# Layer 3: a row of key tiles in two steps of 512 query columns instead of three

## Chip, core and metric

The kernel runs on one core of a Trainium2 chip. The time is the device time of one launch in microseconds; below 3281 us is one run of the whole program. A core has a matrix engine (TensorE, PE in the profile; its weight loads are PEld), a vector engine (VectorE, DVE), a scalar engine (ScalarE, ACT), GpSimd (POOL), a sequencer that issues transfers (SyncE, SP), and DMA engines. Each engine runs its own instructions in order and waits for the others by semaphores. SBUF is the working memory, PSUM the small memory that TensorE writes to, in banks of 512 float32 columns.

## What is computed

Four images of 256 channels and 48 x 48 pixels go through four residual layers: x = x + layer(group_norm(x)). Layers 0 to 2 are convolutions and are not touched. Layer 3 is a linear attention over square windows:

```python
q = sigmoid(Wq x); k = sigmoid(Wk x)        # 8 heads of 32 channels
v = Wv x / |Wv x|                           # per head
for w in (1, 2, 4):                         # windows of 48, 24 and 12 pixels
    ws = Hh // w
    wk = _box(Ik, ws, Hh, Ww)               # sums of k over each query's window
    wkv = _box(Ikv, ws, Hh, Ww)             # sums of k v^T over the same window
    attn = einsum('bdhw,bdfhw->bfhw', q, wkv)
    norm = einsum('bdhw,bdhw->bhw', q, wk)
    outs.append(attn / (norm + 1e-6))
out = Wout concat(outs) + bout
```

## The kernel before

**Tiles.** The image is cut into row blocks of RB = 8 rows (NRB = 6, NB = 384 pixels). A query block is one row block of one image `b` and one half `ct` of the channels (four heads, HG = 4): 48 blocks, in the list `order`. A key tile is one row block `a` times 16 columns (KC), so 128 keys, and a row block has three of them, c = 0, 1, 2 (NKC). A query sees a key tile if the tile lies inside one of its windows, half widths HALVES = 24, 12, 6.

**A step.** `stream` lists every (block, a, c). For each one the kernel does this:

- `scores`: for each of four heads, TensorE multiplies the key tile (32 channels x 128 keys) by the queries that can see it, into a PSUM tile `s` of two banks for two heads; there are two such tiles, and both are used in each step. The queries lie by rows (`qs`, r then w), so the columns that see the tile (`cols_seen`: 40, 48 or 40 of the 48) are cut out of each row: 320 or 384 columns a head.
- `unseen`: a small bfloat16 product adds a large negative number where a query does not see a key of the widest window.
- `masked`: ScalarE applies a relu to the widest window's part, and VectorE multiplies the middle window's part by a 0/1 mask; GpSimd takes the narrowest window's part from the middle one's result. All go to an SBUF tile `sm` (six buffers). If the rows lie whole within the widest window (`rows_whole`), only the strips at its edge (`strips`) are taken here, because the inside comes from sums of k v^T (`state`, `window_state`, `whole`); a middle tile then has two strips of 8 columns on both sides. For the farthest row blocks (distance 3) the whole tile goes through ScalarE for one pair of heads and VectorE for the other.
- `sums`, LAG = 2 steps later: TensorE multiplies `sm` by the values (128 keys x 32 channels) and adds into three PSUM tiles `acc`, one per window, four heads in four groups of 32 columns.

Row blocks are visited nearest first, with near tiles (those that the narrowest window sees) and far ones in turn (`tiles_of`).

**What fills the gaps.** Projections of the next image (`Projection`), prefix sums of k (`k_sums`), the norms (`norms`, `inverse`), key states (`state`), and the output product (`prepare`, `finish`) are generators. After each step `advance(time, pool_time)` lets each of them go on by one piece if the step's spare TensorE time (`bank`, `turn`) or GpSimd time (`pool_turn`) allows it. All of these share one PSUM bank (`ps_m`), one piece at a time. `until` runs them without new steps until something is made: a block's sums may not begin before the block two before it is done. All engines keep program order, so this planner's order is the order on the chip.

**Names in the profile.** A helper records the operations, so nearly all have line 208; they are told apart by tiles: `s`, `sm`, `acc`, `nhi` (norm sums), `nq` (queries for the norms), `pt` (prefix sums), `o` and `stage` (sums of the two channel halves), `rc` (1/norm), `out_ps`, `proj_ps`, `keys_ps`, `kv_ps`, `norm_ps`.

Of the kernel before, what the change touches and what calls it, by code (L numbers as in the profile page):

```python
# [22 lines left out]
P = 128  # L23
# [60 lines left out]
LAG = 2  # L84
HOLD = 1000
# [4 lines left out]
MCOL0 = [max(h, KC) for h in HALVES]  # L90
# [13 lines left out]
def strips(c):  # L104

    (c0, c1), (f0, f1) = cols_seen(0, c), cols_whole(c)
    return [(p0, p1) for p0, p1 in ((c0, f0), (f1, c1)) if p0 < p1]
# [10 lines left out]
def penalties():  # L118

    got = []  # L120
    for c in range(NKC):
        xs = np.concatenate([np.arange(p0, p1) for p0, p1 in strips(c)])
        got.append(((0, c), RB, np.tile(xs[None, :], (RB, 1)), None))
    for da, (r0, r1) in FAR_ROWS.items():
        for c in range(NKC):
            c0, c1 = cols_seen(0, c)
            rs = np.arange(r0, r1)
            got.append(((da, c), r1 - r0, np.tile(np.arange(c0, c1)[None, :], (len(rs), 1)), rs))
    return got


PENALTY_AT, _at = {}, 0
for _key, _nr, _xs, _ in penalties():
    PENALTY_AT[_key] = _at, _xs.size
    _at += _xs.size
# [5 lines left out]
SM_ROOM = 2 * RB * sum(min(W, n) for n in (KC, KC + 2 * HALVES[1], KC + 2 * HALVES[2]))  # L141


def window_masks():
# [5 lines left out]
    for h, nr, m0, ncol in list(zip(HALVES, MROWS, MCOL0, MCOLS))[1:]:  # L150
        qi = np.arange(nr) - h + 1
        qj = np.arange(ncol) - m0
        rows = (qi[None] - h <= ki[:, None]) & (ki[:, None] < qi[None] + h)
        cols = (qj[None] - h <= kj[:, None]) & (kj[:, None] < qj[None] + h)
        ms.append((rows[:, :, None] & cols[:, None, :]).reshape(P, -1))
# [4 lines left out]
    for (da, c), _, xs, rs in penalties():  # L160
        at, n = PENALTY_AT[da, c]
        kx = c * KC + np.arange(KC)[:, None, None]
        costs[RB : RB + KC, at : at + n] = (
            UNSEEN * ~((xs - h <= kx) & (kx < xs + h))
        ).reshape(KC, n)
        if rs is not None:
            ky, ys = da * RB + np.arange(RB)[:, None, None], rs[:, None] + 0 * xs
            costs[0:RB, at : at + n] = (
                UNSEEN * ~((ys - h <= ky) & (ky < ys + h))
            ).reshape(RB, n)  # L170
# [41 lines left out]
def conv_preact_kernel(  # L212
# [104 lines left out]
    def start(job):  # L317
        active.append([step + 1, job])
# [47 lines left out]
    free = {"xr": 2, "xn": 2, "kt": 2, "sq": 2, "vt": 1, "cs": 1, "o": 2, "rc": 2, "res": 2}  # L366

    FETCH = 4
# [22 lines left out]
    class Projection:  # L391
# [14 lines left out]
        def load(self, g, a, n):  # L406
# [7 lines left out]
            xr = self.scr.tile([P, NCT, RB, W], F32, tag="xr", name="xr")  # L414
# [27 lines left out]
        def qk(self, g, a, name, mo):  # L442
# [18 lines left out]
            rows = t.rearrange("p (r c x) -> p c r x", c=NKC, x=KC)  # L461
# [14 lines left out]
        def v(self, g, a, c):  # L476
# [24 lines left out]
            sq = self.scr.tile([P, HEADS, D], F32, tag="sq", name="sq")  # L501
# [14 lines left out]
            for _ in range(4):  # L516
                yield from pool_turn(n, 4)
                pool.tensor_mul(u, t, r)
                pool.tensor_mul(u, u, r)
                pool.tensor_scalar(u, u, -0.5, 1.5, ALU.mult, ALU.add)  # L520
                pool.tensor_mul(r, r, u)
                yield 1
# [1061 lines left out]
    with (  # L1584
# [16 lines left out]
                "p (r c) -> p r c", c=MCOLS[i]  # L1601
# [32 lines left out]
        def k_sums(b, a, mo):  # L1634

            yield from wait_for(("k", b, mo, a))
            kp = kps[mo]
            chans = slice(mo * P, (mo + 1) * P)
            sync.dma_start(
                out=shifted(kp, 0),  # L1640
                in_=kf_d[b][chans, a * NB : (a + 1) * NB].rearrange("p (r x) -> p r x", x=W),
            )
            yield 2 * FETCH
            yield from take("cs")
            cs = scr.tile([P, (RB + 1) * ROW], F32, tag="cs", name="cs", bufs=1)
            n = GAP + RB * ROW
            for i, j in ((0, n // 2), (n // 2, n)):
                dve.tensor_tensor_scan(
                    cs[:, i:j],
                    kp[:, i:j],  # L1650
                    kp[:, 0:1].to_broadcast([P, j - i]),
                    cs[:, i - 1 : i] if i > 0 else 0.0,
                    ALU.add,
                    ALU.add,
                )
                yield 1
            pt = scr.tile([P, NW, RB, W], F32, tag="pt", name="pt")
            for wi, h in enumerate(HALVES):
                dve.tensor_sub(pt[:, wi], shifted(cs, h - 1), shifted(cs, -h - 1))
                yield 1  # L1660
            free["cs"] += 1
            for r in range(RB):
                if r % 2 == 0:
                    yield from pool_turn(NW * W, 2)
                if a > 0 or r > 0:
                    up = pt[:, :, r - 1, :] if r > 0 else carry[:, mo]
                    pool.tensor_add(pt[:, :, r, :], pt[:, :, r, :], up)
            pool.tensor_copy(carry[:, mo], pt[:, :, RB - 1, :])
            yield 1
            sync.dma_start(  # L1670
                out=kb_d[b][:, chans, a * RB : (a + 1) * RB, :].rearrange("w p r x -> p w (r x)"),
                in_=pt.rearrange("p w r x -> p w (r x)"),
            )
            made.add(("kb", b, mo, a))

        def norms(b, rb):
# [4 lines left out]
            def load(ct):  # L1681
# [3 lines left out]
                qf = scr.tile([P, RB, W], F32, tag="nq", name="nq")  # L1685
                sync.dma_start(
                    out=qf.rearrange("p r w -> p (r w)"),
# [30 lines left out]
            for hi, lo, qf in loaded:  # L1718
# [5 lines left out]
                for wi in range(NW):  # L1724
                    yield from pool_turn(NB)
                    pool.tensor_mul(hi[:, wi], hi[:, wi], qf)
# [23 lines left out]
            nr = scr.tile([P, nn], F32, tag="nr", name="nr")  # L1750
# [13 lines left out]
        def load_kv(b, ct, a):  # L1764
# [11 lines left out]
            start(state(b, ct, a))  # L1776
# [40 lines left out]
        def load_q(b, ct, rb):  # L1817
            qs = qp.tile([P, RB, W], F32, tag="qs", name="qs")
            sync.dma_start(
                out=qs.rearrange("p r w -> p (r w)"),  # L1820
# [16 lines left out]
        class Block:  # L1837


            def __init__(self, b, ct, rb, qs):  # L1840
# [3 lines left out]
                    [(a, c) for a, c in self.tiles if seen(wi, a, rb)] for wi in range(NW)  # L1844
# [3 lines left out]
            def scores(self, pr, a, c):  # L1848
                rb = self.rb
                r0, r1 = rows_seen(0, a, rb)  # L1850
                c0, c1 = cols_seen(0, c)
                s = ps_s.tile([P, 2, 512], F32, tag="s", name="s")
                for j in range(2):
                    head = slice((2 * pr + j) * D, (2 * pr + j + 1) * D)
                    pe.matmul(
                        s[:, j, 0 : (r1 - r0) * (c1 - c0)],
                        kvs[self.b, self.ct, a][0][head, c, :],
                        self.qs[head, r0:r1, c0:c1],
                        start=True,
                        stop=False,  # L1860
                    )
                return s[:, :, 0 : (r1 - r0) * (c1 - c0)].rearrange(
                    "p j (r w) -> p j r w", w=c1 - c0
                )

            def unseen(self, ss, a, c):

                whole = rows_whole(a, self.rb)
                at, n = PENALTY_AT[(0 if whole else a - self.rb), c]
                ps = strips(c) if whole else [cols_seen(0, c)]  # L1870
                w, x0 = ps[0][1] - ps[0][0], cols_seen(0, c)[0]
                for pr, s in enumerate(ss):
                    for j in range(2):
                        g = 2 * pr + j
                        rows = slice(g * D, g * D + RB + KC)
                        cost = masks[rows, PEN_AT + at : PEN_AT + at + n]
                        dst = s[:, j, :, ps[0][0] - x0 : ps[-1][1] - x0]
                        if len(ps) == 1:
                            cost = cost.rearrange("p (r w) -> p r w", w=w)
                        else:  # L1880
                            step = (ps[1][0] - ps[0][0]) // w
                            cost = cost.rearrange("p (r s w) -> p r s w", w=w, s=2)
                            dst = dst.rearrange("p r (s w) -> p r s w", w=w)[:, :, ::step]
                        pe.matmul(dst, picks[rows, :], cost, start=False, stop=True)

            def masked(self, a, c, ss):

                rb = self.rb
                all0 = rows_seen(0, a, rb), cols_seen(0, c)
                (r0, r1), (c0, c1) = all0  # L1890
                wis = [wi for wi in range(NW) if seen(wi, a, rb)]
                full = rows_whole(a, rb)
                pieces = {wi: [cols_seen(wi, c)] for wi in wis}
                if full:
                    pieces[0] = strips(c)

                def room():

                    t = smp.tile([P, SM_ROOM], F32, tag="sm", name="sm")
                    at, got = 0, {}  # L1900
                    for wi in wis:
                        nr = rows_seen(wi, a, rb)[1] - rows_seen(wi, a, rb)[0]
                        for p0, p1 in pieces[wi]:
                            n = 2 * nr * (p1 - p0)
                            got[wi, p0] = t[:, at : at + n].rearrange(
                                "p (j r w) -> p j r w", j=2, r=nr
# [3 lines left out]
                    return got  # L1910
# [389 lines left out]
```

## Time and profile before

| | |
|---|---|
| median of 3 runs | 3281.37 us (3277.27 to 3284.92) |
| the profiled execution's own time | 3280.77 us |
| its span in the trace | 3279.0 us, mean TensorE clock 0.968 |
| first and last product of tile `s` | 1380.4 and 3261.4 us |
| last copy of `acc` | begins at 3265.4 us |
| busy share of the span: PE, DVE, ACT, POOL | 89%, 61%, 31%, 45% |
| records of `s`, of its mask products, of `acc` | 5760, 2880, 14976 |
| GpSimd operations on `sm` | 768, 606.9 us |
| VectorE mask operations on `sm` | 1152, 633.1 us |
| ScalarE operations on `sm` | 1680, 559.9 us |

A float32 product leaves two records in the trace, a bfloat16 one leaves one. In a group's line the numbers behind the bar are busy us, mean ns of one, and the engine's idle time just before them with what ended it. Busy time of TensorE overlaps itself: four heads' products run at once in four parts of the array.

### The profile page before, as it was taken

What the parts mean: (1) busy time and instruction counts of PE and PEld (TensorE: products, weight loads), DVE (VectorE), ACT (ScalarE), POOL (GpSimd) and SP (SyncE); (2) the same over time, 40 slices, a digit from 0 to 9 for tenths busy, and PEclk for the clock granted to TensorE, in tenths of its full rate; (3) what the DMA queues carried; (4) which work ended last, traced back from release to release, by engine and by line L of the source; (5) the groups of instructions that cost most, each with busy time, mean ns of one, the idle gap of its engine ahead of it and who ended that gap; (6) DMA issues with size and microseconds to landing.
All of it is one profiled execution on the core that took longest, in us unless ns stands there. A gap on an engine that the chain in (4) does not pass through costs nothing.

```text
span 3279.0 us, 90374 instructions
## 1 busy us (share of the span) xinstructions
PE 2927.0 (89%) x37898; PEld 1845.0 (56%) x37898; DVE 1989.5 (61%) x3571; ACT 1028.7 (31%) x2710; POOL 1476.0 (45%) x2402
## 2 busy tenths in 40 slices
PE   3678999898899978899999999989999999989998
PEld 2456777678676755755544544544455544455444
DVE  7886568648856633666666746665556564444444
ACT  0002210111121053255433344433345433334332
POOL 0000021003002121366899978887546896543433
PEclk9889899999999989899999999999999999999999
DMA  8746513432341253233646645655424555311321
GB/s 268 220 152 189 164 47 119 120 122 78 107 155 55 91 165 120 92 102 125 186 145 177 186 134 172 176 157 167 117 75 125 157 162 152 99 46 36 93 67 53
DMA packets 373099, 424.13 MB, mean 129 GB/s; under 512 B 129075, under 2 KB 328531, under 8 KB 371539
## 3 DMA queue, kind: packets, MB, share of 16 engines
q1 hardware_dynamic: 371491, 416.32, 41.3%
q8 instruction: 298, 4.88, 0.6%
q0 software_dynamic: 144, 1.24, 0.2%
q14 instruction: 110, 0.90, 0.1%
q10 hardware_dynamic: 1056, 0.79, 0.1%
HBM read 288.24 MB, written 131.25 MB: 128 GB/s over the span
## 4 chain that ended last, share of the span: by engine, by line
PE 58%; DVE 12%; POOL 7%; ACT 5%; issue 3%; DMA 3%; SPq 0%; ACTq 0%; POOLq 0%; DVEq 0%
PE s L208 17%; PE cv L208 15%; PE acc L208 12%; PE out_ps L208 5%; PE proj_ps L208 5%; DVE sm L208 4%; ACT sm L208 4%; POOL sm L208 3%; PE ap L208 2%; POOL pt L208 2%; DVE l2v L208 2%; POOL nhi L208 1%; DVE v L208 1%; PE keys_ps L208 1%; DVE x L208 1%
## 5 line engine op out<-in xcount | busy, mean ns | idle before, releaser
L208 DVE TENSOR_TENSOR sm<-s,masks 128x432 f32<-128x432 f32 (+8 forms) x1152 | 633.1, 577 | 551.0 <-PE s L208 477.4
L208 ACT ACTIVATE sm<-s 128x128 f32<-128x128 f32 (+3 forms) x1680 | 559.9, 361 | 903.2 <-PE s L208 708.8
L208 POOL TENSOR_TENSOR sm<-sm,masks 128x336 f32<-128x336 f32 (+8 forms) x768 | 606.9, 811 | 524.2 <-DVE sm L208 520.6
L208 PE MATMUL s<-qs,ks 32*128 32x320 f32 (+3 forms) x5760 | 649.3, 496 | 98.5 <-DVE sm L208 49.4
L208 PE MATMUL acc<-sm,vs 128*32 128x64 f32 (+13 forms) x14976 | 661.6, 303 | 4.4 <-POOL sm L208 4.3
L208 PE MATMUL cv<-vx,wt 128*128 128x288 f32 x2080 | 562.2, 426 | 92.3 <-DVE vx L208 51.2
L208 PEld LDWEIGHTS acc<-sm,vs 128*32 128x32 f32 x14976 | 348.9, 110 | 315.7 <-issue 237.7
L208 PEld LDWEIGHTS cv<-vx,wt 128*128 128x128 f32 x2080 | 404.1, 199 | 214.7 <-issue 54.4
L208 PEld LDWEIGHTS s<-qs,ks 32*128 32x128 f32 x5760 | 260.0, 183 | 397.2 <-ACT sm L208 168.3
L208 POOL MEMSET v<- 128x16 f32 (+1 forms) x120 | 18.5, 215 | 717.8 <-DVE vx L208 631.4
L208 PE MATMUL cv<-v,wl 128*128 128x384 f32 x1152 | 223.9, 354 | 24.3 <-DVE x L208 9.2
L208 DVE TENSOR_SCALAR sm<-s 128x672 f32<-128x672 f32 (+1 forms) x144 | 118.6, 824 | 190.1 <-PE s L208 167.8
L208 PEld LDWEIGHTS cv<-v,wl 128*128 128x128 f32 x1152 | 214.5, 195 | 34.1 <-issue 16.1
L208 PE MATMUL s<-masks 24*128 24x128 bf16 (+4 forms) x2880 | 215.2, 233 | 0.0
L208 POOL TENSOR_TENSOR pt<-pt 128x144 f32<-128x144 f32 x336 | 178.9, 532 | 21.8
L208 POOL TENSOR_TENSOR v<-l2v,v 128x384 fp32r<-128x384 f32 x96 | 109.0, 1166 | 125.3 <-ACT v L208 116.6
L208 POOL TENSOR_TENSOR nhi<-nhi,nq 128x384 f32<-128x384 f32 x144 | 152.6, 1078 | 0.0
L208 PE MATMUL cv<-pad,wl 128*128 128x384 bf16 x864 | 143.6, 328 | 0.0
L208 PEld LDWEIGHTS <-masks 24*128 24x128 bf16 x2880 | 100.8, 93 | 50.9 <-issue 1.0
L208 PE MATMUL out_ps<-o,wout_sb 128*32 128x384 f32 x1152 | 122.2, 492 | 2.3 <-DVE res L208 1.5
L208 PE MATMUL out_ps<-stage,wout_sb 128*32 128x384 f32 x1152 | 121.6, 490 | 1.2 <-DVE stage L208 1.1
L208 PEld LDWEIGHTS <-wl 128*128 128x128 bf16 x864 | 84.0, 97 | 59.8 <-issue 1.3
(174 smaller groups left out, 3375.1 us busy)
## 6 DMA issues: line engine op xcount, KB each, us to landing
wt<-wt SPq DMA_DIRECT2D x48, 768.0 KB
kb_d<-pt SPq DMA_DIRECT2D x48, 576.0 KB
rc<-r_d SPq DMA_DIRECT2D x192, 144.0 KB
nhi<-kb_d SPq DMA_DIRECT2D x120, 192.0 KB
nlo<-kb_d SPq DMA_DIRECT2D x88, 192.0 KB
o_d<-stage SPq DMA_DIRECT2D x24, 576.0 KB
o<-o_d SPq DMA_DIRECT2D x24, 576.0 KB
wl<-wl_d SPq DMA_DIRECT2D x16, 768.0 KB
```

The source lines that it names most:

```text
L208: return lambda *args, **kwargs: self.tc.keep_in_program_order(op(*args, **kwargs))
```

## The change

The query columns of a row block are halved. Step `half` = 0 takes tile 0 (columns 0 to 40) and the left half of tile 1 (columns 0 to 24), step 1 the right half of tile 1 (24 to 48) and tile 2 (8 to 48): 64 columns of 8 rows, 512 score columns a head, one full bank. Queries, `sm`, `acc`, `stage` and masks are held by columns (w then r), so that in a bank the strip of the first tile ends where the strip of the second begins; ScalarE takes both at once. Each window has two pieces in each step, one per key tile.

With it come: q written by columns and read back through a rearranged view where it meets row-ordered data (`nq`, `rc`, `res`); `k_sums` as one job for each `mo` that loads the next row block early; other order and pace of the fillers (`ahead`, FETCH 3, `paced(..., 1)`, fewer pauses in `finish` and in the Newton steps of `v`); other buffer counts (`xr` 1, `vt` 2, `sq` 1, `nr` 1); MIDWAY and WHOLE at steps 3 and 4 of a block instead of 5 and 6; and new constants in the planner's step (GpSimd 3600 ns in place of 2400, TensorE 1200 in place of 900).

```diff
+PARTS = [
+    [(0, *cols_seen(0, 0)), (1, 0, MID)],
+    [(1, MID, W), (2, *cols_seen(0, 2))],
+]
+def parts_seen(wi, half):
+    got = []
+    for c, x0, x1 in PARTS[half]:
+        p0, p1 = cols_seen(wi, c)
+        got.append((c, max(x0, p0), min(x1, p1)))
+    return got
...
-    free = {"xr": 2, "xn": 2, "kt": 2, "sq": 2, "vt": 1, "cs": 1, "o": 2, "rc": 2, "res": 2}
-    FETCH = 4
+    free = {"xr": 1, "xn": 2, "kt": 2, "sq": 2, "vt": 2, "cs": 1, "o": 2, "rc": 2, "res": 2}
+    FETCH = 3
...
-                    pool.tensor_mul(hi[:, wi], hi[:, wi], qf)
+                    pool.tensor_mul(hi[:, wi], hi[:, wi], qf.rearrange("p w r -> p r w"))
...
+            def scores(self, a, half):
+                r0, r1 = rows_seen(0, a, self.rb)
+                ss = [ps_s.tile([P, 2, 512], F32, tag="s", name="s") for _ in range(NPR)]
+                at = 0
+                for c, x0, x1 in PARTS[half]:
+                    n = (x1 - x0) * (r1 - r0)
+                    for pr, s in enumerate(ss):
+                        for j in range(2):
+                            head = slice((2 * pr + j) * D, (2 * pr + j + 1) * D)
+                            pe.matmul(
+                                s[:, j, at : at + n],
+                                kvs[self.b, self.ct, a][0][head, c, :],
+                                self.qs[head, x0:x1, r0:r1],
+                                start=(at == 0),
+                                stop=False,
+                            )
+                    at += n
...
+                def middle(s, room_):
+                    y0, y1 = rows_seen(1, a, rb)
+                    for c, p0, p1 in parts_seen(1, half):
+                        at = offset[c] + (p0 - left[c]) * RB
+                        src = s[:, :, at : at + (p1 - p0) * RB].rearrange(
+                            "p j (x r) -> p j x r", r=RB
+                        )[:, :, :, y0:y1]
+                        times_mask(dve, 1, c, (y0, y1), (p0, p1), room_[1][1, c], src)
+                def widest(engine, s, room_):
+                    n = room_[0].shape[2]
+                    lo, hi = strip_columns(half) if full else (0, n)
+                    if engine is act:
+                        act.activation(room_[0], s[:, :, lo:hi], AF.Relu)
+                    else:
+                        dve.tensor_scalar_max(room_[0], s[:, :, lo:hi], 0.0)
...
-                for c in (1, 0, 2)
+                for half in range(2)
...
-                pool.tensor_mul(o[:, wi], o[:, wi], rcs[0][:, wi])
+                ow = o[:, wi].rearrange("p (w r) -> p w r", w=W)
+                pool.tensor_mul(ow, ow, rcs[0][:, wi].rearrange("p (r w) -> p w r", w=W))
...
+            def divide(wi):
+                sw = stage[:, wi].rearrange("p (w r) -> p w r", w=W)
+                dve.tensor_mul(sw, sw, rc[:, wi].rearrange("p (r w) -> p w r", w=W))
...
-                pool_time = 2400.0 - far_time(*stream[n][:3])
-                time = 900.0 + mask_time(*stream[n][:3]) - sums_time(*stream[n - LAG][:4])
+                pool_time = 3600.0 - far_time(*stream[n][:3])
+                time = 1200.0 + mask_time(*stream[n][:3]) - sums_time(*stream[n - LAG][:4])
```

## The prediction, made before the changed kernel ran

> **What bounds the kernel now.** I read the page's slices first, then the busy time by stretches, then the timeline of a quiet stretch, then the waits, and last the groups by form. The scores of layer 3 (tile `s`) run from 1380.4 us to the end, and TensorE holds 8 or 9 tenths there:
>
> ```profile
> PE   3678999898899978899999999989999999989998
> DVE  7886568648856633666666746665556564444444
> POOL 0000021003002121366899978887546896543433
> ...
> L208 PE MATMUL s<-qs,ks 32*128 32x320 f32 (+3 forms) x5760 | 649.3, 496 | 98.5 <-DVE sm L208 49.4
> L208 PE MATMUL acc<-sm,vs 128*32 128x64 f32 (+13 forms) x14976 | 661.6, 303 | 4.4 <-POOL sm L208 4.3
> ```
>
> A float32 product leaves two records, so four heads make 8 `s` records a step: 5760/8 = 720 steps in about 1885 us (1380.4 to 3265), 2.62 us each. The slices show GpSimd (POOL) full in the middle, which the stretches of 82 us give as numbers (sum, PE, PEld, DVE, ACT, POOL, clock, DMA, GB/s):
>
> ```profile
> 1640.00:1722.00 82.00, 75.54 (x1288) 38.61 (x1284) 53.81 (x86) 26.63 (x82) 78.11 (x118) 1.00 0.49 145
> 1722.00:1804.00 82.00, 76.08 (x1292) 38.77 (x1292) 57.19 (x89) 28.57 (x83) 75.92 (x100) 0.98 0.66 179
> 2952.00:3034.00 82.00, 75.07 (x1476) 43.08 (x1476) 38.22 (x65) 33.37 (x97) 29.88 (x44) 1.00 0.12 36
> ```
>
> So there are two regimes: around 1640 to 1886 us GpSimd is 93% busy, and near the end it is a third busy while TensorE is still short of full. Of the late regime, a step as it runs (start, us, engine, form, count, [idle before]):
>
> ```profile
> 2984.81 0.82 PE L208 MATMUL s<-qs,ks 32*128 32x320 f32 x8 [0.39 <-DVE sm L208]
> 2985.45 0.24 PE L208 MATMUL s<-masks 24*128 24x128 bf16 x4
> 2985.61 0.75 PEld L208 LDWEIGHTS acc<-sm,vs 128*32 128x32 f32 x24 [0.32 <-issue]
> 2985.62 1.10 PE L208 MATMUL acc<-sm,vs 128*32 128x224 f32 x24
> 2985.71 1.12 DVE L208 TENSOR_TENSOR sm<-s,masks 128x432 f32<-128x432 f32 x2 [0.96 <-PE s L208]
> 2986.79 0.91 PE L208 MATMUL s<-qs,ks 32*128 32x320 f32 x8
> 2988.89 0.93 PE L208 MATMUL s<-qs,ks 32*128 32x384 f32 x8
> 2989.64 0.24 PE L208 MATMUL s<-masks 24*128 24x128 bf16 x4
> ```
>
> The reader should see the loop: scores and masks 0.88 us (2984.81 to 2985.69), VectorE 0.90 us after their start and for 1.12 us, then the next scores at 2986.79. TensorE's own work is done just before VectorE, and where it has no other product to do it waits. The waits from 1400 us on (total us, times, longest):
>
> ```profile
> PEld s L208 <- ACT sm L208: 166.0, 282, 2.5
> ...
> PEld s L208 <- DVE sm L208: 80.2, 132, 2.8
> DVE res L208 <- PE out_ps L208: 76.1, 42, 13.0
> ...
> PE s L208 <- DVE sm L208: 46.2, 101, 2.1
> ...
> PE s L208 <- ACT sm L208: 43.8, 128, 1.8
> ```
>
> [...] TensorE is called 93% busy while `s` waits 90 us. I count steps from start to start. [...] each step goes from 32-row to 32-column tiles, and the 0.32 us of "issue" above is there at nearly each of them. [...]
>
> **The change part by part.** A block of queries meets 30 rows of key tiles in each of 8 passes: 240 rows, by distance 128 near (0 or 1), 64 middle (2), 48 far (3). Rows go from three steps to two, 720 to 480 steps; score columns per head and row stay 1024, and so do the sums' columns.
>
> TensorE, scores: 0.88 us for 320 columns and 0.99 for 384 (2988.89 to 2989.88), so 1.7 ns a column and 0.34 us fixed. 512 columns: 0.34 + 0.87 + 0.03 for the wider mask product + 0.05 estimated for the second group of products = 1.29. A row: 0.88 + 0.99 + 0.88 = 2.75 before, 2.58 after; 240 x 0.17 = 41 us less.
>
> TensorE, sums: groups of eight records go from 14976/8 = 1872 to 2240, since every window now has two pieces in a step. A group costs some 0.06 us above its columns (the 24 records above hold 528 columns, 0.90 us, in 1.10 us): 368 x 0.06 = 22 us more[...]: net 8 us more. With the scores, 33 us less. The runs of 3 to 6 rows in a column that the sums now write to PSUM cover some 52,000 columns, 87 us; if those slowed by a quarter, 22 us more. I take 0[...].
>
> Evacuation. The forms:
>
> ```profile
> L208 DVE TENSOR_TENSOR sm<-s,masks 128x448 f32<-128x448 f32 x256 | 148.0, 617 | 88.2 <-PE s L208 87.0
> L208 DVE TENSOR_TENSOR sm<-s,masks 128x312 f32<-128x312 f32 x64 | 30.4, 479 | 25.0 <-PE s L208 21.0 <-POOL vu L208 1.6 <-POOL sm L208 1.1
> L208 POOL TENSOR_TENSOR sm<-sm,masks 128x432 f32<-128x432 f32 x96 | 101.1, 1074 | 81.9 <-DVE sm L208 81.9
> L208 POOL TENSOR_TENSOR sm<-sm,masks 128x210 f32<-128x210 f32 x80 | 50.7, 653 | 36.2 <-DVE sm L208 36.2
> ```
>
> VectorE pays 1.0 ns an element and 0.16 us fixed. A near row took (448 + 624 + 432) elements twice in six operations, and takes the same in eight, some 0.3 us more; ScalarE has four operations of 384 a row in place of eight of 256 or 128, so VectorE ends last. A near step's loop becomes: scores seen by VectorE after 0.90 + 192 x 1.7 ns + 0.1 = 1.33 us, then 2 x (0.617 + 0.47) = 2.17: 3.5 us. TensorE's own work in it is 1.29 + 1.75 = 3.04, so 0.45 us is idle if nothing else is there. Middle: 1.33 + 1.35 = 2.7 against 2.1; far: some 2.85 against 2.35. Before, the same subtraction gives 0.35 us on average (the step at 2984.81: 1.98 us from start to start, 0.88 + 1.10 of work, no loss; far and middle steps run at 1.8 to 2.3 with 1.4 to 1.7 of work).
>
> What counts is how many steps are bare. TensorE's other products (projections, output, norms, key states) are as many as before, at most one as a rule per step; in the two programs' order, 328 of 720 steps hold none before, 130 of 480 after. Idle: 328 x 0.35 = 115 us, against 130 x 0.5 = 65 us and some 8 us in steps with only a short product: 42 us less.
>
> GpSimd: 768 mask operations become 1024 on the same elements. From 653 ns at 210 elements and 1074 at 432, an operation costs 1.9 ns an element and 0.25 us fixed: 256 x 0.25 = 64 us more work. In the late regime it is hidden behind two-thirds idle time; at 93% it is not. There the planner's GpSimd allowance per row is the same (3 x 2400 or 2 x 3600 ns, less more operations), so norms come later. The order shows what is late next: blocks may not begin before the one two back is finished, and where that forces work out, pieces stand in a heap between scores and sums. Before there are 5 such heaps of three or more pieces, one with norm products behind GpSimd work issued in the same heap (2186 to 2202 us: the last addition's longest wait, 13.0 us above). After there are 11, three of them such (steps 92, 122 and 200 of 480; at 92, 26 us of GpSimd work stand between one step's masks and the next's). At 15 us each, 45 - 13 = 32 us more, 10 us for other norms and sums that come behind a fuller GpSimd queue, and 8 us for pieces that follow each other on the one bank: 50 us more.
>
> Strided reads. `nhi` times `nq` (144) and `o` times `rc` (72) on GpSimd now read one operand with steps of 32 or 192 bytes. Bounds: nothing, if the library's operation, which already takes some 2.6 ns an element at 384, is bound elsewhere[...]. I take nothing, and keep the other end as a rival. VectorE's `stage` times `rc` (72) and the last addition (48) are strided too, 0 to 0.4 us each; I take 3 us on the path.
>
> The q sigmoid writes by columns (off the path), loads keep contiguous rows, and the earlier reload of `kp` is hidden by the scan before it: nothing each. Layers 0 to 2 keep their work.
>
> Sum: -33 - 42 + 50 + 3 = -22 us. Against the profiled run's own time, 3280.8 us (span 3279.0 and 1.8 around it, 0.6 below the median of the runs): 3259 us.
>
> **The rivals.** (B) The heaps wait little, because GpSimd catches up in the bare steps ahead of them: the 42 us of GpSimd waits fall away, 3217 us. For: before waits only 13 us there. Against: 93% in the full stretches. (C) Strided reads on GpSimd cost their price: [...] 3294 us, slower. It decides from about 0.2 us an operation (22 us / 216 / one half). Against: no row shows it. (D) The loop of scores and evacuation is longer than 3.5 us, since the first pair's second group now queues behind the second pair's first: 0.12 us on some 200 steps takes the gain, 3282 us.
>
> **How the numbers follow.** Forecast 0.45 with its own range 3235 to 3274; B 0.16; C 0.28; D 0.11. Under 0.2% (6.5 us) this kernel's measurement can't tell from no change. Faster: nearly all of the forecast's cases and B, 0.60; same: D and the edges, 0.13; slower: C, 0.27. The range reaches from B to C with the PSUM term: 3212 to 3307.
>
> **What would show it.** 480 score steps of about 1.3 us unhindered; `PE s` waits under 60 us; norm products waiting for `nhi` 40 us or more, around one eighth, one quarter and 40% of the stage; `nhi<-nhi,nq` at its old 1078 ns (1.3 us or more means C). Wrong if near steps without another product run well over 3.5 us, or if GpSimd never holds TensorE.

## The result and the profile after

The changed kernel takes 3272.98 us (median; 3262.34 to 3285.88), the kernel before 3281.6 us in the same job: a ratio of 0.9971, 95% interval 0.9960 to 0.9983, so 9 us less where 22 were forecast. The sign is right and the size is not, and the experiments show that the forecast's sum held two large errors that partly covered each other.

I cut both profiled executions at three places: the last product of `vx` and `wt` (the end of layer 0's last convolution), the first score and the last sum. The starts of these records give:

| us | before | after |
|---|---|---|
| to the last `vx` product | 1143.2 | 1140.2 |
| from there to the first score | 237.2 | 252.0 |
| the stage: first score to last sum | 1884.5 | 1863.5 |
| the tail, to the end of the span | 14.1 | 16.4 |
| span | 3279.0 | 3272.1 |

So the stage is 21 us shorter, nearly the forecast's number, but 15 us are lost ahead of it and 2 behind it. The page of the kernel after, its slices of the span and its groups:

```profile
PE   3678999899899978889986879998999999999999
POOL 0000021003002130358999968989857888844554
PEclk9889899999999978989998989999999999999999
...
L244 POOL TENSOR_TENSOR sm<-sm,masks 128x352 f32<-128x352 f32 (+11 forms) x1024 | 685.9, 702 | 363.9 <-DVE sm L244 263.1
...
L244 PE MATMUL acc<-sm,vs 128*32 128x128 f32 (+20 forms) x17920 | 626.1, 279 | 36.4 <-POOL sm L244 31.7
...
L244 PE MATMUL s<-qs,ks 32*128 32x192 f32 (+3 forms) x7680 | 594.3, 401 | 41.6 <-ACT sm L244 36.3
...
L244 POOL TENSOR_TENSOR nhi<-nhi,nq 128x384 f32<-128x384 f32 x144 | 176.2, 1243 | 0.0
...
L244 DVE SCALAR_TENSOR_TENSOR res<-out_ps,bout_sb,res 128x384 f32<-128x384 f32 x48 | 42.1, 878 | 128.9 <-PE out_ps L244 128.8
```

Read the first two rows together: TensorE falls to 6, 8 and 7 tenths in the 22nd to 24th slice, in and just behind the slices where GpSimd is at 9 (the 20th to 23rd), and its granted clock is at 8 tenths in the 22nd and 24th (row PEclk). Late in the span TensorE is at 9 throughout. `nhi<-nhi,nq` has risen from 1078 ns to 1243, which the forecast took as unchanged. The stretches in which GpSimd was full before, and the late one (sum, PE, PEld, DVE, ACT, POOL, clock, DMA, GB/s):

```profile
1640.00:1722.00 82.00, 72.59 (x1498) 45.30 (x1492) 58.24 (x107) 25.21 (x51) 76.19 (x123) 1.00 0.59 175
1722.00:1804.00 82.00, 57.00 (x932) 28.07 (x928) 44.94 (x74) 14.56 (x29) 76.27 (x98) 0.88 0.52 144
1886.00:1968.00 82.00, 63.57 (x964) 30.28 (x960) 30.88 (x48) 18.14 (x33) 58.05 (x69) 0.83 0.42 130
2952.00:3034.00 82.00, 77.28 (x1754) 55.48 (x1750) 42.42 (x93) 31.66 (x64) 38.13 (x64) 1.00 0.16 49
```

From 1722 to 1804 us GpSimd is as full as before (76 of 82 us), while TensorE has 57 us in place of 76. Its waits in the stage (total us, times, longest):

```profile
PE s L244 <- ACT sm L244: 34.7, 93, 1.9
PE acc L244 <- POOL sm L244: 31.7, 52, 2.1
PE norm_ps L244 <- POOL nhi L244: 29.5, 18, 10.8
...
PEld norm_ps L244 <- POOL nhi L244: 67.3, 32, 11.5
```

The waits for evacuation (`PE s`) are less than half of what they were, 90 us; in their place the sums wait for GpSimd's masks and the norm products for GpSimd's `nhi`, both 4 to 5 us before. The wait for `nhi` is longer than the row of PE says: the norm products come in pairs, each pair waits for one more `nhi`, and the records of the pair ahead, here often 0.85 us long in place of 0.49 (41 of 288 over 0.8 us, before 8), fill much of that wait. The weight loads of these products (PEld, last row) wait 67.3 us, and in the kernel before 8.1:

```profile
PEld norm_ps L208 <- POOL nhi L208: 8.1, 4, 4.4
```

What GpSimd does meanwhile, in its timeline (start, us, form, count):

```profile
1759.39 4.84 POOL L244 TENSOR_TENSOR pt<-pt 128x144 f32<-128x144 f32 x7
1764.29 0.30 POOL L244 COPY carry<-pt 128x144 f32<-128x144 f32 x1
1764.56 0.99 POOL L244 TENSOR_TENSOR nhi<-nhi,nlo 128x384 f32<-128x384 f32 x1
...
1768.37 3.46 POOL L244 TENSOR_TENSOR nhi<-nhi,nq 128x384 f32<-128x384 f32 x3
1771.79 3.21 POOL L244 TENSOR_TENSOR nhi<-nhi,nlo 128x384 f32<-128x384 f32 x3
1774.97 3.46 POOL L244 TENSOR_TENSOR nhi<-nhi,nq 128x384 f32<-128x384 f32 x3
```

It runs nearly one operation after the other, all of it for norms and key sums, with no mask between. Three products with the strided `nq` take 3.46 us; how much of that is the stride, only a run without it can tell. By sixteenths of the stage (30 steps now, 45 before), the two of steps 90 to 150 (135 to 225 before) went from 251.8 us to 307.0, all others together from 1632.7 to 1556.5: 55 us lost in these steps, 76 gained elsewhere.

A quiet step after, steps of the timeline:

```profile
2985.80 1.26 PE L244 MATMUL s<-qs,ks 32*128 32x192 f32 x14 [0.28 <-ACT sm L244]
...
2987.34 1.48 PE L244 MATMUL acc<-sm,vs 128*32 128x224 f32 x48
2987.39 1.92 DVE L244 TENSOR_TENSOR sm<-s,masks 128x320 f32<-128x320 f32 x4 [1.25 <-PE s L244]
...
2988.97 1.34 PE L244 MATMUL s<-qs,ks 32*128 32x192 f32 x14 [0.15 <-ACT sm L244]
```

From scores to scores 3.17 us. VectorE's four mask operations take 1.92 us and the near sums 1.48, where I had counted 2.17 and 1.75.

### The profile page after: what moved, and what is told of

Read it like the earlier page. It is cut to its first block, busy times and chain, and to the rows that moved or that the text cites. A ratio compares the mean times of both kernels' runs of the same rounds, so it can differ in the third digit from the quotient of the medians.

```text
span 3272.1 us, 98025 instructions
## 1 busy us (share of the span) xinstructions
PE 2902.1 (89%) x41802; PEld 2004.4 (61%) x41802; DVE 2017.0 (62%) x3907; ACT 963.2 (29%) x1894; POOL 1613.6 (49%) x2658
## 4 chain that ended last, share of the span: by engine, by line
PE 51%; POOL 16%; DVE 10%; DMA 3%; ACT 3%; issue 3%; SPq 1%; ACTq 0%; POOLq 0%; DVEq 0%
PE cv L244 15%; PE s L244 13%; PE acc L244 11%; POOL sm L244 6%; PE out_ps L244 5%; PE proj_ps L244 4%; POOL nhi L244 4%; POOL pt L244 3%; PE ap L244 2%; DVE sm L244 2%; DVE l2v L244 2%; ACT sm L244 2%; SPq L244 1%; DVE v L244 1%; POOL vu L244 1%
## 5 line engine op out<-in xcount | busy, mean ns | idle before, releaser
L244 DVE TENSOR_TENSOR sm<-s,masks 128x448 f32<-128x448 f32 (+11 forms) x1536 | 632.6, 468 | 443.7 <-PE s L244 417.3
L244 POOL TENSOR_TENSOR sm<-sm,masks 128x352 f32<-128x352 f32 (+11 forms) x1024 | 685.9, 702 | 363.9 <-DVE sm L244 263.1
L244 ACT ACTIVATE sm<-s 128x384 f32<-128x384 f32 (+2 forms) x864 | 470.5, 545 | 845.3 <-PE s L244 662.2
L244 PE MATMUL acc<-sm,vs 128*32 128x128 f32 (+20 forms) x17920 | 626.1, 279 | 36.4 <-POOL sm L244 31.7
L244 PE MATMUL s<-qs,ks 32*128 32x192 f32 (+3 forms) x7680 | 594.3, 401 | 41.6 <-ACT sm L244 36.3
L244 PEld LDWEIGHTS acc<-sm,vs 128*32 128x32 f32 x17920 | 431.6, 110 | 241.9 <-issue 139.0
L244 PEld LDWEIGHTS s<-qs,ks 32*128 32x128 f32 x7680 | 372.7, 186 | 271.1 <-issue 122.3
L244 PEld LDWEIGHTS cv<-v,wl 128*128 128x128 f32 x1152 | 216.4, 197 | 36.4 <-issue 16.7
L244 DVE TENSOR_SCALAR sm<-s 128x896 f32<-128x896 f32 (+1 forms) x96 | 111.1, 1157 | 186.1 <-PE s L244 161.2
L244 POOL TENSOR_TENSOR nhi<-nhi,nq 128x384 f32<-128x384 f32 x144 | 176.2, 1243 | 0.0
L244 PE MATMUL s<-masks 24*128 24x192 bf16 (+2 forms) x1920 | 172.1, 269 | 0.0
L244 DVE SCALAR_TENSOR_TENSOR res<-out_ps,bout_sb,res 128x384 f32<-128x384 f32 x48 | 42.1, 878 | 128.9 <-PE out_ps L244 128.8
```

The lines of the kernel that those rows point to most:

```text
L244: return lambda *args, **kwargs: self.tc.keep_in_program_order(op(*args, **kwargs))
```

## The experiments

The theory after the result: the change itself gains more than forecast, and gives it back in three places: strided reads on GpSimd, strided operands on VectorE, and a longer stretch ahead of the stage. The rivals: that heaps in the planner's order make the norms late; that the stretch ahead of the stage is one execution's chance. The ratios below are to the kernel before of the same job. In the edits, words in angle brackets stand for a longer expression, and `...` for code left out.

**e1_contig**

```diff
-pool.tensor_mul(hi[:, wi], hi[:, wi], qf.rearrange("p w r -> p r w"))
+pool.tensor_mul(hi[:, wi], hi[:, wi], <qf in the order it lies>)
-pool.tensor_mul(ow, ow, rcs[0][:, wi].rearrange("p (r w) -> p w r", w=W))
+pool.tensor_mul(o[:, wi], o[:, wi], rcs[0][:, wi])
```

> The changed kernel, but GpSimd reads queries and reciprocals in the order in which they lie (nq and rc without a stride, so rows and columns of the output are paired wrongly; nothing else differs). The rival that strided reads cost: nhi<-nhi,nq comes back from 1243 to about 1077 ns and o<-o,rc from 1244 to 1036, 216 x 0.19 = 41 us less GpSimd work in the stage; half of it lay on the path, so the time is 20 us below the changed kernel (0.991 of before), most of it in the fourth and fifth sixteenth of the stage. The theory that the strides are hidden: the durations come back but the time moves by less than 7 us (0.995 to 0.999 of before). Ahead of the stage nothing differs from the changed kernel: the theory that its thinner buffers cost 12 us there expects the first score near 1392 us again; the rival that this was one execution's clock expects anything from 1380 to 1392.

Measured: 3247.18 us, 0.9901 (0.9882 to 0.9921), 23 us below the changed kernel by the ratios. The stage is 1836.0 us, 27.5 less. The groups of its trace in the stage:

```profile
L244 POOL TENSOR_TENSOR nhi<-nhi,nq 128x384 f32<-128x384 f32 x144 | 147.8, 1046 | 0.0
...
L244 POOL TENSOR_TENSOR o<-o,rc 128x384 f32<-128x384 f32 x72 | 72.0, 1024 | 0.0
```

Against 176.2 and 87.8 us these are 44 us less GpSimd work, and nearly two thirds of it lay on the path. Steps 90 to 150 give 11 us of it (307.0 to 296.1), the rest comes in small pieces wherever GpSimd is nearly full. But 296 is still 44 over before, so the strides aren't why these steps are long.

**b1_strided**, the same from the other side:

```diff
 # in the kernel before
-pool.tensor_mul(hi[:, wi], hi[:, wi], qf)
+pool.tensor_mul(hi[:, wi], hi[:, wi], <qf read with steps of 32 bytes>)
-pool.tensor_mul(o[:, wi], o[:, wi], rcs[0][:, wi])
+pool.tensor_mul(ow, ow, <rc read with steps of 192 bytes>)
```

> The kernel before, but GpSimd's 144 products nhi times nq and 72 products o times rc read nq and rc with the strides that the changed kernel has (32 and 192 bytes; rows and columns of the output are paired wrongly). Theory that strided reads lengthen whatever stage GpSimd fills: 0.2 us each, 43 us more GpSimd work, the stage is 10 to 25 us longer than 1885 us, the time 1.003 to 1.008 of before. Rival that they cost only in the changed order, where norms come late: the durations rise by 0.2 us but the time stays within 5 us, 1.000 to 1.0015. Either way this is a second record of the old part ahead of the stage: the theory that the changed kernel is longer there expects 237 us or little more from the last product of vx and wt (1143 us in the kernel before) to the first score; the rival that its 237 was one lucky execution expects 244 to 252 as in the changed kernels.

Measured: 3298.55 us, 1.0053 (1.0043 to 1.0062); the stage 1899.3 us, 14.8 more. `nhi<-nhi,nq` takes 1281 ns, `o<-o,rc` 1233. So the strides cost in the old order too, a third of the work they add, probably because GpSimd is less full there (69% busy in the stage of before, 77% in that of the changed kernel). Ahead of the stage 239.8 us: the 237.2 was no lucky execution.

**e5_vec**

```diff
-dve.tensor_mul(sw, sw, rc[:, wi].rearrange("p (r w) -> p w r", w=W))
+dve.tensor_mul(stage[:, wi], stage[:, wi], rc[:, wi])
-dve.scalar_tensor_tensor(xs, ps.rearrange("p (w r) -> p w r", w=W), ..., xs, ALU.add, ALU.add)
+dve.scalar_tensor_tensor(xs, ps, ..., xs, ALU.add, ALU.add)   # xs = res[:, mo], flat
```

> The changed kernel, but VectorE's 72 products stage times rc and 48 last additions into res read and write without strides, as before the change (rows and columns of the output are paired wrongly). By the forecast's step 3 us come back; by the trace 72 x 0.29 + 48 x 0.26 = 33 us less VectorE work, 2.3 us of it in the tail after the last sums. Theory that VectorE's strides lie beside other work: 2 to 5 us, 0.9955 to 0.9965 of before. Rival that they hold blocks up as GpSimd's do: 10 us or more, 0.994 or less.

Measured: 3262.95 us, 0.9938 (0.9921 to 0.9956), 11 us below the changed kernel; with the intervals of both, 4 to 18. In the trace the stage is 7.1 us shorter and the tail 0.7. The ratio meets the rival, the trace lies between the two expectations. VectorE's strides aren't hidden. Where they wait shows only in part: `PE out_ps` waits 6.2 us for `stage` times `rc` in the changed kernel and 4.2 here.

**b2_first**

```diff
 # in the kernel before, first projections only
-xr x2, four advances from load to use, vt x1, sq x2, an advance between Newton steps, q by rows
+xr x1, three advances, vt x2, sq x1, none between Newton steps, q's sigmoid by columns
```

> The kernel before, but the first projections are those of the changed kernel: one xr buffer, three advances to its use, two vt, one sq, no advance between Newton steps, and the queries' sigmoid written by columns (so the first image's queries lie in the wrong order). Theory that this part costs the changed kernel some 10 us ahead of the stage: the time is 1.002 to 1.004 of before, and the stretch from the last vx product to the first score grows from 237 us to 244 to 252. Rival that it is chance or that the stage differs: 0.999 to 1.001.

Measured: 3293.06 us, 1.0022 (1.0007 to 1.0037), 7 us. Its stage is that of before (1885.5 us), and from the last `vx` product to the first score it takes 250.8 us. ScalarE's and VectorE's waits there:

```profile
ACT xn L208 <- DMA xr<-x_d: 9.4, 5, 3.7
...
DVE ss L208 <- ACT sq L208: 28.7, 14, 8.7
```

Before, the first was 1.2 us in one wait, the second 14.8. In every run with the thin pace ScalarE waits 5.3 to 9.9 us for these loads, in those with the old pace at most 1.4. That what layer 0 still asks of ScalarE comes later for this is my reading; the traces show that VectorE's `x` waits 46.5 us for the products `ap` here and in the changed kernel, 30.9 before and 33.8 in e3, at the old pace. With 250.8 us on the old kernel, the chance theory falls.

**e2_qrows** and **e3_first** take this cost apart in the changed kernel: only the sigmoid as before, or only the pace (two `xr`, four advances, an advance between Newton steps).

> The changed kernel, but in the first projections (those ahead of layer 3) the sigmoid of the queries writes by rows as before (so the first image's queries lie in the wrong order). Theory that ScalarE's strided write is what made the part ahead of the stage longer: 12 writes go from 0.88 to 0.49 us, the waits of proj_ps for sg shrink, the first score comes 5 us or more earlier than 1392, and the time is 0.996 or less of before. Theory that it is the buffers: under 2 us, 0.997.

> The changed kernel, but the first projections have the old pace: two xr buffers, four advances between the load and its use, an advance between Newton steps. Theory that the thin buffers cost the 12 us ahead of the stage: ACT xn no longer waits for the xr loads (9.9 us to about 1), the first score comes back to 1380 to 1384 us, and the time is 8 to 12 us below the changed kernel, 0.994 of before. Rival that the strided sigmoid or the clock did it: the first score stays at 1388 to 1394 us and the time at 0.997.

Measured: 0.9966 (0.9950 to 0.9982) and 0.9959 (0.9944 to 0.9975); neither can be told from 0.9971 by its time alone. The traces say more. From the last `vx` product to the first score:

| first projections | us |
|---|---|
| old pace, q by rows, in the old order: before, b1 | 237.2, 239.8 |
| thin, q by columns: after, e1, e4, e5, e6, b2 | 252.0, 244.0, 249.2, 249.5, 251.9, 250.8 |
| thin, q by rows: e2 | 245.6 |
| old pace, q by columns: e3, c1 | 241.7, 242.6 |
| old pace, q by rows: e7 | 241.6 |
| old pace, 12 copies more on ScalarE: c2, c4, c5 | 253.4, 254.5, 254.2 |
| the same copies on GpSimd: c6 | 242.2 |

The pace is worth some 8 us, and no run separates its parts (the second `xr`, the fourth advance, the pause between Newton steps); the sigmoid by columns lies within the 8 us by which the same code differs between executions, and its share stays open.

**e4_dve0**

```diff
-pool.tensor_mul(hi[:, wi], hi[:, wi], ...)
+(pool if b > 0 else dve).tensor_mul(hi[:, wi], hi[:, wi], ...)
```

> The changed kernel, but the first image's products nhi times nq (36 of them) run on VectorE in place of GpSimd. Theory that GpSimd's load in the first third of the stage makes the norms late and the steps 90 to 150 long (55 us over before): 36 x 1.24 = 45 us less GpSimd work there, VectorE takes some 25 us more beside it, the waits of the norm products for nhi fall from 29.5 us to under 15, and the time is 20 to 35 us below the changed kernel, 0.988 to 0.991 of before. Rival that those steps are long by the single bank and the order alone: under 7 us, or slower, as VectorE's evacuation is what most steps wait for.

Measured: 3258.56 us, 0.9936 (0.9921 to 0.9952), 11 us below the changed kernel, about half of what the theory asked; the stage is 18.3 us shorter. Steps 90 to 150 fall from 307.0 to 260.0 us, and the weight loads of the norm products wait 29.3 us for `nhi` in place of 67.3, but steps 30 to 90 and 150 to 210 get 28 us longer. Less GpSimd work shortens those steps; VectorE pays for it (1.2 us each there).

**e6_allow6**

```diff
-pool_time = 3600.0 - far_time(*stream[n][:3])
+pool_time = 6000.0 - far_time(*stream[n][:3])
```

> The changed kernel, but the planner's GpSimd allowance in a step is 6000 ns less the far products in place of 3600; nothing is computed otherwise. In the order the heaps at steps 92 and 200 are gone, the one at 122 falls from 13 pieces to 5, and the bare steps from 130 to 107. Theory that the allowance, which the change left at its old size per row while every near row got more GpSimd operations, is what makes the norms late: the 55 us that steps 90 to 150 lie over before shrink by half or more, and the time is 20 to 40 us below the changed kernel, 0.985 to 0.991 of before. Rival that GpSimd is simply full there, so that work planned earlier only holds up the masks in front of the sums (PE acc on POOL sm from 31.7 us to 60 or more): within 8 us of the changed kernel, 0.995 to 0.9995.

Measured: 3283.64 us, 1.0003 (0.9991 to 1.0015): 10 us slower than the changed kernel, slower than either expectation; the stage is 1875.2 us. Steps 90 to 150 do fall, to 264.6 us, and all others rise by 54 us. Its waits:

```profile
PE acc L244 <- POOL sm L244: 59.2, 62, 4.3
...
PE norm_ps L244 <- POOL nhi L244: 9.6, 17, 1.9
```

The wait moved from the norms (29.5 to 9.6 us, by the weight loads 67.3 to 27.2) to the masks in front of the sums (31.7 to 59.2), as the rival said. The heaps that I had counted in the order are where GpSimd's lateness shows; without them it shows elsewhere.

**c1_reorder** and **c2_two_q** compute the whole result without the strided products.

```diff
 # c1 and c2: reciprocals by columns, old pace in the first projections
-act.copy(ns, ps[0 : D * NW, 0:NB])
+act.copy(ns.rearrange("p (w r) -> p r w", w=W), ps[...].rearrange("p (r w) -> p r w", w=W))
 # c1: behind the load of nq, in norms
+act.copy(qf, qc.rearrange("p w r -> p r w"))
 # c2: where q is made; both t and kt are stored, nq is loaded from t's array
+act.copy(kt.rearrange("p (w r) -> p r w", w=W), t.rearrange("p (r w) -> p r w", w=W))
```

> The changed kernel with its strides moved to ScalarE and the old pace of the first projections: ns is copied out of PSUM by columns (24 copies), so that rc comes by columns and o times rc and stage times rc need no stride, and nq is copied into rows by ScalarE (48 copies) ahead of its products; the two xr buffers and four advances of the kernel before in the first projections. Theory: GpSimd's 27 us come back (e1), VectorE's and the pace's 5 to 8 us too, less 5 us for 72 strided copies on ScalarE: 24 to 32 us below the changed kernel, 0.987 to 0.990 of before. Rival that ScalarE's copies, which now stand between the load and the product, make the norms as late as before: 0.993 to 0.996.

> As c1_reorder, but the queries by rows for the norms come from a second array: the sigmoid writes rows as in the kernel before, ScalarE copies them by columns at once (from its own result, in place of a copy behind a load), both are stored, and nq is loaded by rows. Theory that c1 gave most of the gain away because ScalarE's copy stood behind a load in front of evacuations: PE s on ACT sm falls back from 59 to about 35 us, and the stage comes to 1830 to 1840 us; the time is 0.986 to 0.990 of before. Rival that ScalarE's own 0.9 us for a strided copy costs as much wherever it stands: 0.991 to 0.993.

Measured: c1 3260.21 us, 0.9921 (0.9899 to 0.9944), stage 1857.4 us; c2 3252.84 us, 0.9908 (0.9887 to 0.9929), stage 1834.2 us. In c1 `PE s` waits 59.3 us for ScalarE, the longest 6.8 us; in c2 35.7, the longest 1.8. c1 lies between its theory and its rival. The copy seems to cost more where it stands behind a load; but c2 also makes 12 of the 48 copies ahead of the stage, so up to 11 us of the 23 between the stages may be that. c2's stage came to where it was expected, but its 12 copies in the first projections (0.88 us each) gave 11 us back ahead of the stage (table above), which I hadn't expected, and its ratio lies just above what the theory asked.

**c4_q_allow** (c2 with e6's edit) and **c5_q_dve_allow** (c4 with e4's):

> c2_two_q with the GpSimd allowance of 6000 ns. If strides and heaps are two separate costs, the gains of e6 and c2 add: 0.972 to 0.982 of before. If both are only GpSimd's load in the first third, the second adds little: within 5 us of the better of the two.

> c4_q_allow with the first image's 36 products nhi times nq on VectorE. If GpSimd is still what bounds the first third (45 us less of its work there): 5 to 15 us below c4. If not, VectorE's longer queue makes it equal or up to 8 us slower.

Measured: 0.9903 (0.9886 to 0.9921) and 0.9901 (0.9883 to 0.9919). Neither adds anything to c2 that the measurement can tell (stages 1834.9 and 1837.8 us, for c2's 1834.2). With 44 us less for GpSimd to do, neither another order of its work nor moving 36 products to VectorE helps. Whether GpSimd no longer sets the time there, or VectorE loses what GpSimd gains, these runs don't separate.

**e7_all**, e1, e2, e3 and e5 together:

> The changed kernel with all three costs taken away at once: GpSimd's strided reads (as e1), VectorE's strides (as e5), and the first projections at the old pace with the queries' sigmoid by rows (as e2 and e3 together; rows and columns of the output are paired wrongly). If the three are separate costs their gains add: 27 us (e1), 8 to 10 us (e5) and 8 us ahead of the stage (b2): the stage comes to some 1828 us and the time to 0.983 to 0.986 of before. What is left is then what the change without its strides gives: 47 to 55 us, twice the forecast's 22. If GpSimd's and VectorE's strides were one cost seen twice (each waiting for the other at their shared work), the stage stays at 1834 us or more and the time at 0.987 or more.

Measured: 3228.27 us, 0.9842 (0.9822 to 0.9862); the stage 1831.1 us, 241.6 us ahead of it, the tail 15.7. In the stage e1 and e5 alone gave 27.5 and 7.1, together 32.4 us: separate costs. Without them and at the old pace the change is worth 52 us. No run separates the 512-column steps from what came with them in the stage (the order of the fillers, the buffers, the planner's constants); that scores and sums fill less of TensorE (below) speaks for the steps.

**c6_two_q_pool**

```diff
 # c2, in the first projections
-act.copy(kt..., t...)
+pool.tensor_copy(kt..., t...)
```

> c2_two_q, but in the first projections the copy of the queries by columns runs on GpSimd in place of ScalarE. Theory that the part ahead of the stage is set by ScalarE's queue (in c2 its 12 more copies of 0.7 us make it 253 us from the last vx product to the first score, although the pace is the old one): it comes back to 240 to 245 us, and the time falls 8 to 12 us below c2, 0.987 to 0.989 of before. Rival that it is the loads or the chip's clock: 250 us or more, 0.9905.

Measured: 3239.07 us, 0.9873 (0.9852 to 0.9894): the fastest kernel here that computes the whole result, 42 us below before and some 32 below the changed kernel. Ahead of the stage 242.2 us, 11 less than c2 with the same loads and with the 12 copies, 0.88 us each on GpSimd too, off ScalarE: what ScalarE is given here lengthens this stretch about one for one. (The 0.7 us of the expectation is the mean of a group that holds the 12 copies of k, 0.51 us each, as well.)

## Why the forecast's size was wrong

**The step that failed first** is "Strided reads ... I take nothing, and keep the other end as a rival". The products took 0.20 to 0.22 us more each (1243 against 1046 ns, 1244 against 1024), 44 us of GpSimd work, and 27 us of it were on the path (e1). This is rival C's mechanism, at the 0.2 us an operation from which I had said it decides. The reason I gave for nothing, that the operation might be bound elsewhere, had no row behind it, and neither had C's price. C's time of 3294 us didn't come, because TensorE's term was wrong the other way.

**"VectorE 3 us"** was mis-sized: 8 us in the trace of e5, 11 by its ratio. The rows measured 790 to 1179 ns (`stage<-stage,rc`) and 616 to 878 (`res`), inside my bounds of 0 to 0.4 us (0.26 us each of it goes with the strides in e5); it is the share on the path that I took too small.

**"The q sigmoid writes by columns (off the path)" and "Layers 0 to 2 keep their work"** failed as a statement on time. The work is the same, but a thinner pace (one `xr`, three advances) puts waits for loads at the head of ScalarE's queue: 7 us by b2's ratio, 10 by e7's trace. My step named neither the fewer buffers nor who else shares ScalarE in the first projections.

**"TensorE ... 33 us less"** was too little, and covered the others. Counting each moment once, records of `s` with its masks fill 673.7 us of the stage before and 622.6 after (51 less, for the forecast's 41: an unhindered step takes 1.23 us, not 1.29), records of all products into `acc` 685.2 and 664.5 (21 less, for 8 more, in which 14 us taken off for 240 fewer steps were my estimate and stand in no trace). The 0.06 us that I charged for each of 368 more groups of products isn't there: the 48 records of the near sums hold 743 columns, 1.26 us at 1.7 ns, and end in 1.48 us, 0.21 us above for six groups; before it was 0.20 us for three. The runs of 3 to 6 elements in PSUM cost nothing that shows, as taken: at full clock the next group starts 185 ns after one of 108 columns in runs of 4, and 192 ns after one of 112 in runs of 8 (medians), 1.71 ns a column in both.

**"Idle 42 less" and "GpSimd 50 more"**, net 8 more, came out as some 21 more in e7, where nothing else disturbs: its stage is 53.4 us shorter, 74 from TensorE's records (51 of scores, 23 of sums). The first term was about right: `PE s` waits fell from 90 us to 35, in e7 to 33. The second was right in its places and too small. In the changed kernel 57 of the 67.3 us that the norm products wait for `nhi` stand at steps 92, 122 and 200 (16.7, 23.8 and 16.6 us), the three heaps that I had put at 15 us each; in e7 it is 51 us. The sums wait for masks beside that, 31.7 us against 4.3 before (21.7 in e7), more than the 10 I had left for it.

What makes the heaps dear isn't settled. GpSimd's load is one part: the 1024 mask operations take 79 us more than the 768 (64 forecast), and with less work for GpSimd while the first image's norms are due those steps are shorter (e4). The order is another: at step 122 GpSimd itself stands still for 11.0 us, until a load of `nlo` lands that is issued in the same heap, and in e1 and e7 for 11.3 and 11.4, one reason why e1 takes only 5 of 48 us off that step. The theory of a full GpSimd has no place for this. GpSimd's waits for such loads in the changed kernel's stage (total us, times, longest):

```profile
POOL nhi L244 <- DMA nlo<-kb_d: 16.3, 9, 11.0
```

Before there was one, of 5.3 us. TensorE's clock is a third: it was at half for 17.1 of the 39.0 us of step 92, 27.3 of the 47.6 of step 122 and 13.7 of the 27.1 of step 200. Yet e6, which takes the heaps of steps 92 and 200 out and makes the third smaller, is 10 us slower: no run here takes the loss away without one elsewhere.

Put together by the traces: -22 forecast, -41 for TensorE's records, +13 for the waits, +27 and +5 for the strides of GpSimd and VectorE, +10 for the first projections make -8 us; the two profiled spans differ by 6.9.

Of the rivals, B (heaps wait little) and D (a loop over 3.5 us) were wrong: the 71 near steps without another product take 3.14 us in the median. C was right in its mechanism and wrong in its total.

## What to carry to other kernels

The new layout took 74 us off TensorE's records (e7), and other readers and writers of the arrays paid for it: 27 us by GpSimd's strides (e1), 7 by VectorE's (e5). List each operand whose step changes, and where no trace has a row for it, put a price in the forecast, not in a rival, if the engine that pays is full. Moving a full engine's work in time only moved the wait here (e6: 20 us less for the norms, 28 more for the masks); what helped was less work for it (e1: 44 us less, the stage 27.5 us shorter), and a strided copy did best where the data is born, on an engine that had no one waiting behind it (c6: 242.2 us ahead of the stage, where the same copies on ScalarE made it 253.4). A buffer or a pace that is saved in one stage must be checked in each stage that shares the code: here it cost 7 to 10 us in the first projections.

## What the runs showed of the chip

GpSimd's product of 384 elements took 0.20 us more with a second operand of 32-byte steps (1243 ns in the changed kernel, 1046 in e1), and 0.22 us more with 192-byte steps (1244 and 1024). ScalarE paid more for a strided write of as many elements: the sigmoid out of PSUM went from 0.49 to 0.87 us, the copy of `ns` from 0.48 to 0.86 (c2), and a copy by columns within SBUF took 0.88 (c2) where the copy of k, in runs of 16, took 0.51. TensorE's granted clock was either full or half in every record of before and of the changed kernel. In the stage it was at half for 37 us before and 100 in the changed kernel, and TensorE was busy in 30 and 68 us of these. From 1700 to 2050 us the mean clock was 0.98 before, 0.93 in the changed kernel and 0.94 in e7. In the changed kernel 80 of the 100 us lie at the stage's start and at steps 6, 92, 122 and 200, its four longest. At half clock the second of two passes of a norm product starts 0.64 us after the first, at full clock 0.31. So the 38 us more of work at half clock are some 19 us lost, an estimate from these starts; what lowers the clock, no run here separates. Over the whole span the mean clock of the profiled executions was 0.952 to 0.959 with the new order and 0.963 to 0.968 with the old. And the stage repeats well between executions of the same code (1863.5, 1860.6 and 1860.7 us in after, e2 and e3), while the stretch from the last `vx` product to the first score differs by up to 8 us (244.0 to 252.0) and the part ahead of it by 16 (1138.6 us in e2 to 1154.8 in e4): a cost of a few us there needs several traces.
